# Tail pairs of a mixture of experts added to their nodes by accumulating scatters, with the gathers of the other pairs moved beside them

## The chip, the cores and the metric

The kernel runs on one core of one Trainium2 chip. The metric is the time of one execution on the device, in microseconds. The kernel before takes 3260.33 us (median of 14 runs, 3238.46 to 3288.77). The engines are named as the profile names them: PE (TensorE matmuls), PEld (its weight loads), DVE (VectorE), ACT (ScalarE), POOL (GpSimd), SP (SyncE, which here only issues DMAs).

## What is computed

A block of a graph network over 6250 nodes of 256 features (float32) with 100000 edges. Cut to its outline:

```python
xn = _layernorm(x)
x = x + _L0_gnn_ref(xn, edge_index, ...) + _L0_mix_ref(xn[None], ...)[0]
x = x + _L0_ffn_ref(_layernorm(x)[None], ...)[0]

# _L0_gnn_ref: relu(gcn) and relu(gat); each is a segment sum over the edges of rows fetched by source
# _L0_mix_ref: linear attention, 8 heads of 64
# _L0_ffn_ref:
gate_scores = x @ Wg + bg
_, idx = jax.lax.top_k(gate_scores, 2)               # two of 8 experts for every node
mask = jax.nn.one_hot(idx, 8).sum(axis=-2)
h = gelu(einsum('td,edh->teh', x, W1) + b1)          # H = 512
y = einsum('teh,ehd->ted', h, W2) + b2
out = einsum('ted,te->td', y, mask)                  # the two experts' rows are added, unweighted
```

The change concerns the last line: each node's output is its row `x` plus the rows that its two experts return.

## The kernel before

The nodes lie in NB = 49 blocks of P = 128 rows (the last has 106). Most of the time goes to the two graph layers and the mix: POOL fetches rows of neighbours by indirect DMA, PE adds them up per block of destination nodes. None of that is edited, except for the size of one ring of buffers.

The second graph layer finishes blocks one after another, and the class `Experts` works on finished blocks inside it. `finish` computes a block's `x2` and stores it in the array x2d in memory; groups of blocks are then normalised (`normed`), gated, and every node gets two slots, one in the region of each of its experts. `put` (L774) scatters the normalised rows to their slots in the array xs, one indirect DMA for each block and each of the two experts, 98 in all, issued by POOL.

A *pair* is 256 consecutive rows of one expert's region (a pair of 128-row tiles). At most 56 pairs can be needed, and at least 49 (`NPAIR`, `SURE`). For each pair:

- `pick` (DVE) chooses which pair is full, on small tables on the device; its number goes into `pairs`.
- `load` (SP) loads its rows `xg` (256 KB) and its expert's two weight matrices `w1q`, `w2q` (512 KB each).
- `enter` (PE, DVE) transposes the rows, `inner` (PE, ACT) makes the hidden layer with its gelu, `outer` (PE, DVE) multiplies back, half by half, and adds the bias into `yb` (L897). `yb` has two buffers.
- SP stores `yb` as pair number q of the array ys (L903).

The layer's order is written out by hand, slot by slot: each slot issues its gathers, some of the experts' products from the list `todo` (with a budget) and the results that are due. `add` and `after` file a step with a lag in slots. When the layer ends, `order.close()` ends that regime, and `rest` runs: what is left, issued as a plain program that the scheduler of the framework orders at build time by the dependencies between the steps. Each engine then executes its instructions in that fixed order. 36 pairs are picked inside the layer; 20 are left to `rest`, the tail.

`rest` writes rows of zeros behind the last row of each region (SP, L926), so that a pair that is not full reads zeros, and picks and computes the remaining pairs. `turn` (L959) turns each node's slot in xs into a place in ys: pairs were taken in an order that only the device knows, so DVE compares each slot's pair with the 56 entries of `pairs` (L974), multiplies by the entry's number (L978) and sums (L979), for 49 blocks at a time, twice. Then for each block: SP loads `x2d` into `o` (L943), POOL fetches the two rows of each node from ys (L946, 98 indirect DMAs), DVE adds them to `o` (L956) and SP stores the block (L957). Every one of these gathers waits for every store of a pair:

```python
for store in self.stores:
    tc.add_manual_dep(back.ins, store.name, ..., reason="every pair is stored")
```

The graph layers' gathered rows lie in `xres`, an SBUF tile with a place for every block, and in a second tile `ring`. After the layer neither is used in the kernel before.

## Time and profile before

| what | us |
|---|---|
| median of 14 runs | 3260.33 (3238.46 to 3288.77) |
| profiled execution, its own time | 3260.22 |
| span of that execution | 3258.4 |
| busy PE, DVE, ACT, POOL in the span | 2078.2, 1475.8, 755.0, 1594.0 |
| granted PE clock, mean | 0.813 |
| start of the last scatter of rows (L774) | 2914.8 |
| first and last issue of the tail's 20 stores (L903) | 2930.8, 3107.8 |
| first of the 98 gathers (L946) | 3111.0 |

How to read what follows. The page gives the busy time of each engine over the whole span and in 40 slices. The view of windows gives, for stretches that one chooses, each engine's busy time with its number of instructions, the clock that PE was granted (1.00 is full), the mean share of time in which the 16 DMA engines were busy, and the rate that they moved. In the view of groups a line names the source line, the engine, the operation, the tile written and the tile read, their shapes, the number of instructions, then busy microseconds in all, mean nanoseconds of one, and the idle time ahead of them with what ended it. The timeline gives the start of each instruction, its duration, and in brackets how long its engine had been idle and what released it. Averages over the span say little here, since the kernel's end consists of stages with different limits.

### The profile page before, as it was taken

The page shows a single profiled execution, that of the slowest core. Times are in us where ns is not written, and L with a number is a line of the kernel's source. Part 1 is how long each engine was busy: PE and PEld are TensorE (multiplying, and loading weights), DVE is VectorE, ACT ScalarE, POOL GpSimd, SP SyncE. Part 2 cuts the span into 40 slices and gives each one's busy share as a digit, 9 for nine tenths or more (in the row PEclk, how much of TensorE's full clock was granted, in tenths as well). Part 3 has the DMA queues.
Part 4 walks back from the last instruction along what each step waited for, and adds up shares of the span by engine and source line. Part 5 has one row for each costly group of instructions (what it writes and reads, how often), then busy time and mean ns, then how long its engine had stood idle before and what let it go on. Part 6 is the DMA issues. An engine that isn't in the chain of part 4 may idle for free. (4 is left out here: it accounts for less than half of the span.)

```text
span 3258.4 us, 34185 instructions
## 1 busy us (share of the span) xinstructions
PE 2078.2 (64%) x9260; PEld 1530.1 (47%) x9261; DVE 1475.8 (45%) x5122; ACT 755.0 (23%) x1914; POOL 1594.0 (49%) x1753
## 2 busy tenths in 40 slices
PE   3572766776678675642474557786886878678710
PEld 2451444454445454532353335564665657457610
DVE  6221433443433323363654555475655656552322
ACT  3230111222222110011111223342433434221100
POOL 1036666666563625626056666555665565210056
PEclk9686888888889887875687778897988889789865
DMA  3443333333334365634254454565556555335455
GB/s 110 123 149 96 103 98 95 99 101 98 91 116 138 110 182 157 181 111 139 73 155 115 131 156 153 173 190 149 183 175 185 159 170 154 105 127 199 153 160 165
DMA packets 299242, 450.27 MB, mean 138 GB/s; under 512 B 44666, under 2 KB 225566, under 8 KB 298879
## 3 DMA queue, kind: packets, MB, share of 16 engines
q0 software_dynamic: 77184, 210.12, 22.9%
q1 hardware_dynamic: 202690, 220.25, 21.3%
q10 hardware_dynamic: 19165, 17.60, 1.8%
q8 instruction: 78, 1.28, 0.2%
q14 instruction: 125, 1.02, 0.1%
HBM read 377.19 MB, written 71.40 MB: 138 GB/s over the span
## 5 line engine op out<-in xcount | busy, mean ns | idle before, releaser
L1554 POOL DMA_INDIRECT xres<-ytab,srcidx x698 | 691.6, 991 | 560.9 <-PE agg L1558 241.1
L1748 POOL DMA_INDIRECT xres<-ftab,srcidx x455 | 449.6, 988 | 356.7 <-PE agg L1882 153.7
L1558 PE MATMUL agg<-xres,S 128*128 128x256 f32 x1396 | 363.4, 413 | 20.2 <-issue 19.9
L1558 PEld LDWEIGHTS agg<-xres,S 128*128 128x128 f32 x1396 | 293.8, 212 | 111.8 <-issue 61.7
L1748 POOL DMA_INDIRECT ring<-ftab,srcidx x243 | 236.3, 972 | 131.5 <-issue 52.8
L1882 PE MATMUL agg<-xres,PW 128*128 128x257 f32 x910 | 273.1, 441 | 30.5 <-issue 15.8
L870 PE MATMUL px<-xT,w1q 128*128 128x256 f32 x896 | 243.1, 425 | 60.8 <-DVE xT L858 32.1
L1875 ACT ACTIVATE PW<-S,z 128x128 f32<-128x128 bf16 x698 | 225.0, 393 | 194.3 <-DVE S L1858 61.9
L434 DVE TENSOR_REDUCE var<-sq 128x16 f32<-128x1024 f32 x49 | 59.8, 1220 | 406.1 <-ACT sq L432 351.0
L870 PEld LDWEIGHTS px<-xT,w1q 128*128 128x128 f32 x896 | 184.0, 213 | 99.0 <-DVE xT L858 36.0
L1882 PEld LDWEIGHTS agg<-xres,PW 128*128 128x128 f32 x910 | 192.9, 220 | 67.3 <-issue 20.2
L892 PE MATMUL px<-w2q,hT 128*128 128x256 f32 x896 | 215.2, 391 | 14.3 <-ACT hT L877 5.9
L946 POOL DMA_INDIRECT yg<-ys,part x98 | 96.3, 983 | 236.7 <-issue 229.9
L774 POOL DMA_INDIRECT xs<-xn,to_i x98 | 100.3, 1023 | 220.3 <-DVE slot L751 194.1
L427 PE MATMUL kv<-wkvT,xnT 128*128 128x512 f32 x392 | 203.1, 666 | 0.1
L892 PEld LDWEIGHTS px<-w2q,hT 128*128 128x128 f32 x896 | 170.0, 194 | 43.8 <-ACT hT L877 6.8
L877 ACT ACTIVATE hT<-px,b1T 128x256 f32<-128x256 f32 x224 | 95.5, 472 | 323.0 <-PE px L870 200.9
L1782 PE MATMUL pm<-Q,lift_i 128*128 128x512 bf16 (+1 forms) x200 | 77.4, 387 | 139.3 <-DVE mt L1794 97.6
L453 PE MATMUL dots<-kk,vv 128*128 128x128 f32 x392 | 66.9, 323 | 142.3 <-DVE vv L446 76.7
L897 DVE TENSOR_TENSOR yb<-px,fb 128x256 f32<-128x256 f32 x112 | 44.6, 421 | 243.2 <-PE px L892 145.9
L1794 DVE TENSOR_REDUCE mt<-pm 128x1 f32<-128x384 f32 (+1 forms) x201 | 122.1, 608 | 42.8 <-remote 18.9
L1882 PE MATMUL agg<-ring,PW 128*128 128x257 f32 x486 | 133.4, 415 | 3.5 <-issue 3.5
(359 smaller groups left out, 3313.4 us busy)
## 6 DMA issues: line engine op xcount, KB each, us to landing
w1q<-in_L_ffn_W_dram SPq DMA_DIRECT2D x56, 512.0 KB
w2q<-in_L_ffn_W_dram SPq DMA_DIRECT2D x56, 512.0 KB
xg<-xs SPq DMA_DIRECT2D x56, 256.0 KB
ys<-yb SPq DMA_DIRECT2D x56, 256.0 KB
F<-ftab SPq DMA_DIRECT2D x14, 899.5 KB
Y<-ytab SPq DMA_DIRECT2D x14, 896.0 KB
xnT<-xnTd SPq DMA_DIRECT2D x98, 128.0 KB
xres<-ytab,srcidx POOLq DMA_INDIRECT x698
```

What stands on the lines that cost most here:

```text
L427: nc.tensor.matmul(kv[:, s, :], xnT[:, k, :], wkvT[:, k, s * INNER : (s + 1) * INNER], start=(k == 0), stop=(k == 1),)
L774: put = nc.gpsimd.indirect_dma_start(out=xs[:, :], out_offset=bass.IndirectOffsetOnAxis(ap=to_i[:n, j, k : k + 1], axis=0), in_=bt["xn"][k ...
L870: nc.tensor.matmul(ph, w1q[:, k, c * P : (c + 1) * P], xT[:, k, :], start=(k == 0), stop=(k == 1))
L877: nc.scalar.activation(hT[:, c0 + c, :], ph, AF.Gelu, bias=self.b1T[:, c0 + c, bass.ds(e, 1)], scale=1.0)
L892: nc.tensor.matmul(py, hT[:, c, j * P : (j + 1) * P], w2q[:, c, :], start=(c == 0), stop=(c == HC - 1))
L946: back = nc.gpsimd.indirect_dma_start(out=yg[:n, :], out_offset=None, in_=ys[:, :], in_offset=bass.IndirectOffsetOnAxis(ap=self.slot[:n, j ...
L1554: nc.gpsimd.indirect_dma_start(out=R, out_offset=None, in_=ytab[:, :], in_offset=bass.IndirectOffsetOnAxis(ap=srcidx[:, t : t + 1], axis=0),)
L1558: nc.tensor.matmul(sums[b], hot[s][:, t - t0, :], R, start=(t == first[b]), stop=(t == first[b + 1] - 1))
L1748: nc.gpsimd.indirect_dma_start(out=ch["R"][c], out_offset=None, in_=ftab[:, :], in_offset=bass.IndirectOffsetOnAxis(ap=srcidx[:, ch["t0"] ...
L1794: nc.vector.tensor_reduce(ch["mt"][:, q : q + 1], ch["pm", q][:, :w, :].rearrange("p c e -> p (c e)"), AX.X, ALU.max)
L1875: nc.scalar.mul(PW[:, c - c0, :], ch["S", q][:, c - c0, :], ch["z"][:, c : c + 1])
L1882: nc.tensor.matmul(ch["pa"], ch["PW", q][:, c - c0, :], ch["R"][c][:, 0 : D + 1], start=(c == 0), stop=(c == ch["C"] - 1),)
```

## The change

The tail is the pairs that are picked after the layer; `rest` calls their first number `cut` (the constant FEW = 37 is an upper limit on the pairs picked in the layer).

- The rows of a pair in the tail aren't stored to ys. Each half (128 rows) is added to its nodes' rows in x2d, by an indirect DMA from POOL with `compute_op=ALU.add`. So that the node of a row is known, every row of xs gets a 257th column with the node's number (ACT copies it in `normed`), and DVE copies that column of the pair's `xg` into a tile `whose` with four buffers. Rows of zeros behind a region carry numbers of 256 spare rows at the end of x2d.
- Two such scatters may touch the same row, so each waits until the one before has landed.
- Only the first `cut` pairs are stored in ys, with one pair of zeros behind them. `turn` works on `cut` columns instead of 56; a slot whose pair isn't among them gets the pair of zeros.
- The gathers from ys wait for the stores before the cut only. They go into `xres`, the first row of a node straight (`sums`), the second through `yg` and an add of DVE. They are issued a few at a time between the scatters (`self.backs`), the rest after them.
- At the end 13 steps of four blocks each load x2d, add `sums` and store.
- The ring of the layer has 26 rows of its own instead of 27, for the space.

```diff
+    FEW = 37
...
-    xs = dram.tile([NX * RG, D], FP, name="xs")
-    ys = dram.tile([NPAIR * PAIR, D], FP, name="ys")
+    xs = dram.tile([NX * RG + PAIR, D + 1], FP, name="xs")
+    ys = dram.tile([(NPAIR + 1) * PAIR, D], FP, name="ys")
...
-    x2d = dram.tile([NR, D], FP, name="x2d")
+    x2d = dram.tile([NR + PAIR, D], FP, name="x2d")
...
-            xn = self.fp.tile([P, D], FP, name="xn", bufs=2 * GB + 2)
+            xn = self.fp.tile([P, D + 1], FP, name="xn", bufs=2 * GB + 2)
+            i = bt["i"][k]
+            nc.scalar.copy(xn[:, D:], self.nodes[:, i : i + 1])
...
-            if self.waiting == 2 or len(self.puts) < need:
+            if self.waiting == 2 or len(self.puts) < need or (self.cut is None and self.taken == self.few):
                 return self.after(1, lambda: self.pick(need))
...
-            xg = fp.tile([P, 2, D], FP, name="xg")
+            xg = fp.tile([P, 2, D + 1], FP, name="xg")
...
+                if self.cut is not None and q >= self.cut:
+                    self.whose[q] = self.fp.tile([P, 2], I32, name="whose", bufs=4)
+                    nc.vector.tensor_copy(self.whose[q], xg[:, :, D])
...
+                if q in self.whose:
+                    nc.gpsimd.indirect_dma_start(
+                        out=x2d[:, :], out_offset=bass.IndirectOffsetOnAxis(ap=self.whose[q][:, j : j + 1], axis=0),
+                        in_=yb[:, j, :], in_offset=None, compute_op=ALU.add,
+                    )
+                    for back in self.backs[:4]:
+                        back()
+                    del self.backs[:4]
+                    return
                 if j == 0:
                     return
                 store = nc.sync.dma_start(ys[q * PAIR : (q + 1) * PAIR, :].rearrange("(j p) d -> p j d", p=P), yb)
...
         def rest(self, tp):
+            self.cut = self.taken
+            none = tp.tile([P, 4, D + 1], FP, name="none")
+            nc.vector.memset(none, 0.0)
+            for j in range(4):
+                nc.vector.tensor_scalar(none[:, j, D:], pcol, float(NR + j % 2 * P), None, op0=ALU.add)
+            nc.sync.dma_start(xs[NX * RG :, :].rearrange("(j p) d -> p j d", p=P), none[:, 0:2, :])
+            nc.sync.dma_start(x2d[NR:, :].rearrange("(j p) d -> p j d", p=P), none[:, 0:2, 0:D])
+            store = nc.sync.dma_start(
+                ys[self.cut * PAIR : (self.cut + 1) * PAIR, :].rearrange("(j p) d -> p j d", p=P), none[:, 0:2, 0:D]
+            )
...
-            while self.taken < NPAIR:
+            for _ in range(8):
                 self.clock += 1
                 self.products(6.0)
                 self.results()
             self.turn(tp)
+            sums = xres[:, :, 0:D]
+            for i in range(NB):
+                for j in range(2):
+                    self.backs.append(lambda i=i, j=j: self.back(tp, sums, i, j))
             self.drain(6.0)
-            for i in range(NB):
-                n = rows(i)
-                o = tp.tile([P, D], FP, name="o", bufs=4)
-                nc.sync.dma_start(o, x2d[i * P : (i + 1) * P, :])
...
+            for back in self.backs:
+                back()
+            XO = 4
+            for i in range(0, NB, XO):
+                n = min(XO, NB - i)
+                o = tp.tile([P, XO, D], FP, name="o", bufs=4)
+                nc.sync.dma_start(o[:, :n, :], x2d[i * P : (i + n) * P, :].rearrange("(j p) d -> p j d", p=P))
+                nc.vector.tensor_tensor(o[:, :n, :], o[:, :n, :], sums[:, i : i + n, :], op=ALU.add)
...
+        def back(self, tp, sums, i, j):
+            n = rows(i)
+            to = tp.tile([P, D], FP, name="yg", bufs=4) if j else sums[:, i, :]
+            back = nc.gpsimd.indirect_dma_start(
+                out=to[:n, :], out_offset=None, in_=ys[: (self.cut + 1) * PAIR, :],
+                in_offset=bass.IndirectOffsetOnAxis(ap=self.slot[:n, j * NB + i : j * NB + i + 1], axis=0),
+            )
+            for store in self.stores:
+                tc.add_manual_dep(back.ins, store.name, ..., reason="every pair before the cut is stored")
+            if j:
+                nc.vector.tensor_tensor(sums[:n, i, :], to[:n, :], sums[:n, i, :], op=ALU.add)
...
         def turn(self, tp):
+            n = self.cut
...
-            same = tp.tile([P, NB, NPAIR], BF, name="same")
+            same = tp.tile([P, NB, n], BF, name="same")
...
-            NR1, NR2 = NB * RW // GW, 27
+            NR1, NR2 = NB * RW // GW, 26
```

## The prediction

> **What bounds the kernel now.** The page's slices first. The first 85% of the span is the layers' work, and the change hardly touches it; what it reorders begins when the layer's last gathers end, near 2808 us. So I cut the rest with the view of windows at the places where the engines change.
>
> ```profile
> core 0: us, PE busy (x) PEld busy (x) DVE busy (x) ACT busy (x) POOL busy (x), PEclk, DMA share, GB/s
> 2808.00:2887.00 79.00, 69.67 (x383) 56.35 (x382) 47.11 (x190) 32.30 (x94) 0.00 (x0) 0.94 0.29 94
> 2887.00:2930.00 43.00, 21.94 (x89) 17.93 (x90) 26.14 (x209) 5.12 (x10) 9.64 (x10) 0.68 0.48 156
> 2930.00:3098.00 168.00, 137.96 (x611) 113.44 (x610) 50.68 (x178) 29.12 (x68) 0.00 (x0) 0.94 0.53 175
> 3098.00:3111.00 13.00, 8.48 (x40) 6.55 (x38) 2.28 (x6) 1.90 (x4) 0.01 (x1) 1.00 0.32 101
> 3111.00:3247.00 136.00, 0.00 (x0) 0.00 (x0) 40.33 (x96) 0.00 (x0) 94.56 (x97) 0.51 0.62 181
> 3247.00:3258.00 11.00, 0.00 (x0) 0.00 (x0) 1.20 (x3) 0.00 (x0) 1.76 (x1) 0.50 0.20 53
> ```
>
> Two stages follow each other with nothing shared: 181 us in which PE multiplies the last pairs and POOL is empty, then 147 us in which POOL fetches and PE is empty. The seam is one wait: every gather waits for the last store of a pair.
>
> ```profile
> L903 SPq DMA_DIRECT2D ys<-yb x20: 360/431/881, 2930.8 to 3107.8; - x20
> ```
>
> Twenty pairs are stored there: the seventh at 2975.3, the seventeenth at 3070.8, so 9.55 us a pair, 4.8 us a half, set by PE (138 of 168 us busy). Then the gathers, in the timeline:
>
> ```profile
> 3110.99 0.98 POOL L946 DMA_INDIRECT yg<-ys,part  x1 [195.23 <-issue]
> 3112.28 0.97 POOL L946 DMA_INDIRECT yg<-ys,part  x1 [0.31 <-issue]
> 3113.55 0.95 POOL L946 DMA_INDIRECT yg<-ys,part  x1 [0.30 <-issue]
> 3113.77 0.43 DVE L956 TENSOR_TENSOR o<-yg,o 128x256 f32<-128x256 f32 x1 [6.01 <-DMA yg<-ys,part]
> ```
>
> One gather costs POOL 0.95 us and 0.30 us before the next, 1.25 in all (with its stalls on o the mean is 136/97 = 1.40). Issue to first use is 3113.77 - 3110.99 = 2.78 us: the only round trip of an indirect DMA seen alone here, and the nearest row to a link of the new chain.
>
> ```profile
> L974 DVE TENSOR_TENSOR same<-pairsb,mine 128x2744 bf16<-128x2744 bf16 x2 | 6.0, 3010 | 0.0
> L979 DVE TENSOR_REDUCE place<-same 128x49 f32<-128x2744 bf16 x2 | 6.0, 3006 | 0.0
> L978 DVE TENSOR_TENSOR same<-same,pairsb 128x2744 bf16<-128x2744 bf16 x2 | 3.1, 1575 | 0.0
> L897 DVE TENSOR_TENSOR yb<-px,fb 128x256 f32<-128x256 f32 x40 | 15.5, 420 | 102.8 <-PE px L892 102.8
> ```
>
> **The change, part by part.** *In the layer.* The limit of 37 doesn't bind: in the order built from either program 36 pairs are picked when the layer ends. So 20 pairs are the tail, and the layer keeps its picks. New there: 49 ACT copies of a column (a fraction of a microsecond each; ACT is busy 32 of 79 us at the layer's end, and each is ready before its DVE norm), rows of 1028 instead of 1024 bytes in the 98 scatters of L774 and the pair loads, and one ring slot of 75 less (a gather may be asked for one slot, about 1.3 us, later). I take 0: POOL's waits on PE (L1748) and ACT's idle time cover them. Without that cover: 49 x 0.2 = 10 us, an estimate.
>
> *Removed.* The 20 stores of the tail (0.43 us of SP each, beside PE), the seam, the 49 loads and 49 stores of 128 KB, and 20/56 of the slot table: DVE's 2 x (3.01 + 1.58 + 3.01) = 15.2 us become 9.7 at 36 columns. But that table now lies amid pair work, and the first gather needs it.
>
> *Added.* 40 accumulating scatters, each held by the landing of the one before and by DVE's yb; POOL's queue waits with it, the gathers behind it too. DVE gets 20 small copies of node numbers and 49 adds of gathered rows (0.43 us each, 21 us) that stood behind the seam before: it was busy 51 of 168 us, so their time fits, but an add that waits for its gather (up to 2.8 us) holds the yb and xT of a pair behind it; PE is ahead by then, so 0. SP gets three stores of zeros, POOL nothing else. In the built order POOL runs: the layer's 10 last puts, 14 scatters (7 pairs), then one stretch of 98 gathers with 12 scatters (6 pairs) among them, in runs of 4 gathers and three runs of about 20, then the last 14 scatters (7 pairs). yb has two buffers, so PE cannot get more than two pairs ahead of POOL's scatters: behind a run of 20 gathers (25 us) PE stands.
>
> *The link.* Let L be the time from one scatter to the next in the chain. No row has an accumulating DMA. Lower bound 2.8, the gather's round trip; upper 5.6, twice it, since each row is read as well as written. I take the middle, 4.2: the gather moves the same bytes, but doesn't write where it has read.
>
> A rule speaks against the change here. The Trainium skill ("Collectives: The Full Stack", Why ReduceScatter is half of AllGather) says an add on the way needs two source reads, two descriptors per chunk, and so runs at half the rate of a copy (measured ratio 1.93). No row of this trace shows it; applied to the whole round trip it would make L 5.4 and the sum below about 3296.
>
> *Stations, on the clock of the profiled span.*
> 1. First gather. Scatters begin at 2931 as the stores did: 2931 + 14 x 4.2 = 2989.8; by the other path, seventh pair 2975.3 + table 9.7 + one link 4.2 = 2989.2. So 2990 (2988 at L = 2.8, 3009 at 5.6).
> 2. The stretch is POOL's: 110 x 1.25 = 138, and 12 x 0.4 = 5 for scatters dearer to issue (an estimate between 0 and the 0.95 of a second issue): 143, to 3133. The chain is no limit in it (12 links, 50 us). PE gets six pairs, 57 us, in 143 us: some 85 us are lost against before.
> 3. The last seven pairs. Two lie ready in yb: 4 x 4.2 = 17. Five come at PE's pace: 48. To 3198. From L = 4.8 the chain is the slower one: 14 x 5.6 = 78. PE was three fifths idle, and the windows show its clock at 0.68 where it is half busy against 0.94 where it is full; at 0.81 in between the 48 us become 56: +8, to 3206 (from 0).
> 4. Landing of the last scatter: one link, 3210.
> 5. The final stage. 13 loads of 512 KB, an add each (4 x 0.43 = 1.7 us), 14 stores, all behind the last scatter: 12.8 MB. The best 20 us in the tail move 308 GB/s, which makes 42; the gathers' stage made 181, which makes 71. Large blocks and nothing between are nearer the first: 260, 49 us. Around it: first load 5 (o waits up to 5.2), one add 1.7, the last store 5.2 (the last add ends at 3253.2, the span at 3258.4): 12. To 3271.
> 6. The profiled execution is 3260.22 for a span of 3258.4, and the median 3260.33: +1.9. Sum: **3273**.
>
> So the 150 us behind the last store (3108 to 3258) become 65, and the last pair ends 98 us later, at 3206: a loss of 13.
>
> One more rule, beside the sum: the skill ("DMA: Bandwidth & Descriptors", Rules for kernel authors) says that an accumulating DMA beside another access of the same bytes can lose a write, hence one must wait for the other. The trace of before cannot show this; the built order obeys it, with a wait in every scatter. Were it not needed, L would be one issue, 1.3 to 1.7 us, and the sum about 3255, since PE and POOL set the rest.
>
> **The rivals.**
> - *The chain sets the pace.* L above 4.8 us. At 5.6: 3009 + 143 + 78 + 6 + 61 + 1.9 = 3299 (the chain hides the clock's loss); each further microsecond adds 29, so 6.5 us gives 3325. For it: a read and a write in series, and transfers of weights and rows beside them (DMA share 0.53). Against: PE's 4.8 us a half hides all below it.
> - *An add at a copy's price.* L = 2.8 and no dearer issue: 2988 + 138 + 59 + 8 + 3 + 61 + 1.9 = 3259: no change. PE's starvation and the saved stage cancel. Nothing in the trace prices the add, so nothing is against it but the bytes.
> - *Faster: POOL's stretch is shorter.* If the 0.30 us between gathers goes, since more are out at once to different buffers, 98 x 0.30 = 29 us go from station 2: 3244. It decides from 0.23 us a gather (3250). Against: the gap is there after scatters and gathers alike. For: these gathers go into tiles that are free, without the waits on o.
> - *The gathers are hidden after all* would need PE to run on: 13 pairs in the stretch instead of 6, seven x 9.6 = 67 us less, 3206. The two yb buffers exclude it in the built order.
>
> **How the numbers follow.** A difference of 0.3% (10 us) is about what a measurement of this kernel can tell from none: 3250 to 3270 is the same. My case (3262 to 3295) 0.48, of which 0.10 fall below 3270; the chain 0.22, all slower; the copy's price 0.13, the same; the short stretch and anything else to that side 0.17, faster. So faster 0.17, same 0.23, slower 0.60. Range: the low end has L = 2.8, no dearer issue, no loss of clock, 308 GB/s: 2988 + 138 + 59 + 3 + 54 + 1.9 = 3244. The high end has the chain's 3299, with 181 GB/s (+22) 3321, and half a microsecond more of L (+14): 3335. Beyond them about 0.1 on either side.
>
> **What would show it.** Right: no PE work for about 20 us at a time between 2990 and 3133 with POOL at its 1.25 us; PE waiting on yb for POOL's scatter; 20 pairs of the tail ending near 3200; a last stage of 60 us without POOL; 36 columns in the table (128x1764). Wrong: scatters over 4.8 us apart where POOL has nothing else (the chain), or a PE that works through the gathers' stretch. What would break the sum altogether: a layer that ends other than at 2887, or x2d loads that start before the last scatter.

## The result, and the profile after

The changed kernel takes 3295.83 us (median of 10 runs, 3285.18 to 3311.17) against 3257.6 us for the kernel before in the same comparison: ratio 1.0122, interval 1.010 to 1.0144, so 38 us slower. The forecast was 13 us slower, in a range of 3244 to 3335: the direction and the range held, the size was a third of the measured one.

Its profiled execution has a span of 3286.1 us. Executions of one program differ by some 20 us in the layers already (the first layer, which nothing of the change touches, ended at 1406 us in this profile and at 1428 in the one before), so from here on times in the tail are counted from the start of the layer's last aggregation matmul: 2885.7 us in the profile before, 2858.3 in this one. I call the time from there to the end the tail. It was 372.7 us and is 427.9: 55 us more; the 17 us between that and the 38 measured must be gained ahead of it, in the layers. Three more profiles of the changed kernel gave 426.1, 426.4 and 428.5.

The view of windows over the tail of the changed kernel, cut where the engines change:

```profile
core 0: us, PE busy (x) PEld busy (x) DVE busy (x) ACT busy (x) POOL busy (x), PEclk, DMA share, GB/s
2858.00:2990.00 132.00, 79.34 (x313) 64.49 (x313) 58.07 (x354) 15.53 (x35) 31.32 (x24) 0.74 0.57 154
2990.00:3156.00 166.00, 56.93 (x195) 43.94 (x194) 28.40 (x77) 8.76 (x20) 114.57 (x110) 0.65 0.50 134
3156.00:3239.00 83.00, 57.17 (x242) 46.55 (x241) 10.89 (x30) 12.63 (x28) 21.68 (x14) 0.85 0.44 100
3239.00:3286.00 47.00, 0.00 (x0) 0.00 (x0) 15.13 (x13) 0.00 (x0) 0.00 (x0) 0.50 0.85 273
```

The stages are the ones that were forecast. Seven pairs go ahead of the first gather (14 scatters); then come 98 gathers and 12 scatters in 166 us, with PE busy a third of the time; then the last seven pairs in 83 us; then 47 us of loads and stores. Beside the forecast, in microseconds after the layer's last aggregation:

| | forecast | profile |
|---|---|---|
| first gather | 104 | 132 |
| length of POOL's stretch | 143 | 166 |
| last seven pairs, with the last landing | 77 | 83 |
| last stage | 61 | 47 |
| tail | 385 | 428 |

The groups of the tail that answer to the rows shown of before:

```profile
L918 POOL DMA_INDIRECT x2d<-yb,whose x40 | 62.7, 1567 | 157.0 <-DVE yb L912 75.0 <-DMA x2d<-yb,whose 28.5 <-DVE whose L874 19.7
L1012 DVE TENSOR_TENSOR xres<-yg,xres 128x256 f32<-128x256 f32 (+1 forms) x49 | 20.2, 423 | 84.2 <-DMA yg<-ys,part 82.2 <-issue 2.0
L1030 DVE TENSOR_TENSOR same<-pairsb,mine 128x1764 bf16<-128x1764 bf16 x2 | 4.0, 1990 | 0.0
L1035 DVE TENSOR_REDUCE place<-same 128x49 f32<-128x1764 bf16 x2 | 4.0, 1980 | 0.0
L1034 DVE TENSOR_TENSOR same<-same,pairsb 128x1764 bf16<-128x1764 bf16 x2 | 2.1, 1073 | 0.0
```

The table has 36 columns (36 x 49 = 1764) and takes 10.1 us, near the 9.7 worked out. The new row is the scatter: 1.57 us of POOL each against 0.98 for a gather, and 157 us in which POOL stood ahead of one. The timeline shows its links. First two where little else is loaded, then the first ones of the tail:

```profile
3212.28 1.54 POOL L918 DMA_INDIRECT x2d<-yb,whose  x1 [3.46 <-DVE yb L912]
3216.84 1.54 POOL L918 DMA_INDIRECT x2d<-yb,whose  x1 [3.02 <-DVE xT L870]
3221.41 1.54 POOL L918 DMA_INDIRECT x2d<-yb,whose  x1 [3.02 <-DMA x2d<-yb,whose]
...
2903.32 1.61 POOL L918 DMA_INDIRECT x2d<-yb,whose  x1 [15.22 <-DVE yb L912]
2912.89 1.56 POOL L918 DMA_INDIRECT x2d<-yb,whose  x1 [7.97 <-DVE xT L870]
2920.37 1.54 POOL L918 DMA_INDIRECT x2d<-yb,whose  x1 [5.91 <-DMA x2d<-yb,whose]
2929.29 1.54 POOL L918 DMA_INDIRECT x2d<-yb,whose  x1 [7.37 <-DVE yb L912]
2938.99 1.54 POOL L918 DMA_INDIRECT x2d<-yb,whose  x1 [8.16 <-DVE yb L912]
```

3212.28 to 3216.84 is 4.56 us. The first four links are 9.6, 7.5, 8.9 and 9.7 us. The releaser in the brackets is only the semaphore that came last; the packets of the transfers tell what the waits are made of. A quiet scatter's first packet starts 2.1 us after the issue begins and its last ends at 3.4; for that of 2903.32 it is 5.2 and 8.5. In all four of these links the next half lay ready in yb before the last packet had ended. The window from 2903.3 to 2912.9 has the DMA engines full, with weights being loaded, at 272 GB/s; the quiet one from 2943.5 to 2948.0 has 29 GB/s.

And the break in POOL's stretch, in the timeline of POOL, ACT and PE:

```profile
3062.15 0.94 POOL L1001 DMA_INDIRECT yg<-ys,part  x1 [0.30 <-issue]
3077.41 1.60 POOL L918 DMA_INDIRECT x2d<-yb,whose  x1 [14.32 <-DVE yb L912]
...
3062.03 0.47 ACT L892 ACTIVATE hT<-px,b1T 128x256 f32<-128x256 f32 x1 [69.94 <-remote]
...
3040.05 5.49 PE L885 MATMUL px<-xT,w1q 128*128 128x256 f32 x12 [2.82 <-issue]
3062.56 2.08 PE L885 MATMUL px<-xT,w1q 128*128 128x256 f32 x4 [17.01 <-issue]
```

POOL ends a run of 21 gathers and then waits 14.3 us for a pair that isn't there. PE's last 12 matmuls before it are on record from 3040 to 3045.5, but ACT, which waits for these products, starts only at 3062.03, when the run of gathers ends. A second wait, of 11.2 us, lies behind the last gather (3155.8 to 3167.0), so in the time of the last seven pairs.

The last stage, in the timeline and in a row of the view of windows:

```profile
3238.56 1.52 SPq L987 DMA_DIRECT2D o<-x2d  x3
3242.47 1.23 DVE L988 TENSOR_TENSOR o<-o,xres 128x1024 f32<-128x1024 f32 x1 [16.35 <-DMA o<-x2d]
```

```profile
3245.00:3275.00 30.00, 0.00 (x0) 0.00 (x0) 11.21 (x10) 0.00 (x0) 0.00 (x0) 0.50 1.00 324
```

From the first load to the end it takes 47.5 us. From 3245 to 3275 the loads and stores move 324 GB/s, with the DMA engines full.

### The profile page after: what moved, and what is told of

Same layout as the page of the kernel before. It is cut to its first block, busy times and chain, and to the rows that moved or that the text cites. A ratio compares the mean times of both kernels' runs of the same rounds, so it can differ in the third digit from the quotient of the medians.

```text
span 3286.1 us, 34111 instructions
## 1 busy us (share of the span) xinstructions
PE 2111.6 (64%) x9260; PEld 1553.4 (47%) x9261; DVE 1465.4 (45%) x5104; ACT 759.6 (23%) x1962; POOL 1653.6 (50%) x1794
## 5 line engine op out<-in xcount | busy, mean ns | idle before, releaser
L1806 POOL DMA_INDIRECT xres<-ftab,srcidx x464 | 457.2, 985 | 361.5 <-PE agg L1940 156.2
L885 PE MATMUL px<-xT,w1q 128*128 128x256 f32 x896 | 253.1, 441 | 87.5 <-DVE xT L870 37.2
L1806 POOL DMA_INDIRECT ring<-ftab,srcidx x234 | 227.6, 973 | 129.7 <-issue 49.6
L907 PE MATMUL px<-w2q,hT 128*128 128x256 f32 x896 | 225.4, 403 | 71.9 <-DVE yb L912 38.2
L885 PEld LDWEIGHTS px<-xT,w1q 128*128 128x128 f32 x896 | 192.5, 222 | 130.0 <-DVE xT L870 43.1
L1940 PEld LDWEIGHTS agg<-xres,PW 128*128 128x128 f32 x928 | 195.0, 218 | 59.1 <-issue 14.7
L918 POOL DMA_INDIRECT x2d<-yb,whose x40 | 62.7, 1567 | 157.0 <-DVE yb L912 75.0
```

What stands on the lines that cost most here:

```text
L885: nc.tensor.matmul(ph, w1q[:, k, c * P : (c + 1) * P], xT[:, k, :], start=(k == 0), stop=(k == 1))
L907: nc.tensor.matmul(py, hT[:, c, j * P : (j + 1) * P], w2q[:, c, :], start=(c == 0), stop=(c == HC - 1))
L1806: nc.gpsimd.indirect_dma_start(out=ch["R"][c], out_offset=None, in_=ftab[:, :], in_offset=bass.IndirectOffsetOnAxis(ap=srcidx[:, ch["t0"] ...
L1940: nc.tensor.matmul(ch["pa"], ch["PW", q][:, c - c0, :], ch["R"][c][:, 0 : D + 1], start=(c == 0), stop=(c == ch["C"] - 1),)
```

## The experiments

The sets ran on several chips. On one of them (the runs e1_plain, e2_nogather, e3_late, e4_order) the kernel before takes 2700.6 us, on the others 3233 to 3258; ratios are compared within a set only. The tail hardly depends on it where both were tried: 411.1 and 411.2 us for e3, 381.4 and 380.8 for e4, 331.8 and 328.7 for e2. So the tails are what I compare, and after them the ratios. The kernel before was profiled once; its tail is that of the first set.

| run | last scatter | tail | ratio to the kernel before, interval |
|---|---|---|---|
| kernel before | (last store 222) | 373 | 1 |
| changed, four profiles | 374 to 377 | 426 to 428.5 | 1.0122, 1.010 to 1.0144; 1.0137, 1.009 to 1.0184; 1.0135, 1.0097 to 1.0173; 1.0171, 1.0105 to 1.0236 |
| e1_plain | 326 | 376 | 1.002, 0.9997 to 1.0043 |
| e2_nogather | 279, again 277 | 332, 329 | 0.9845, 0.9808 to 0.9882; again 0.9797, 0.9756 to 0.9838 |
| e3_late | 268, again 268 | 411, 411 | 1.0186, 1.0153 to 1.0218; again 1.010, 1.0059 to 1.0142 |
| e4_order | 330, again 329 | 381, 381 | 1.0043, 1.0017 to 1.0069; again 0.9988, 0.9949 to 1.0026 |
| e5_yb4 | 374 | 425 | 1.0159, 1.0114 to 1.0203 |
| e6_end | (last store 232) | 377 | 0.9954, 0.9922 to 0.9985 |
| e7_early | 328 | 379 | 0.9961, 0.9928 to 0.9995 |
| e8_pair | 314, again 312 | 366, 365 | 0.9924, 0.9895 to 0.9954; again 0.9941, 0.9913 to 0.9968 |
| e9_pair_nogather | 253 | 305 | 0.9736, 0.9701 to 0.9771 |
| e11_noadd | 367 | 419 | 1.0114, 1.0077 to 1.015 |
| e12_ring | (last store 221) | 370 | 0.995, 0.9924 to 0.9976 |

My theory after the result was that two things hold the pairs: the gathers in POOL's queue (theory A), and the chain of scatters, which the forecast had thought hidden (theory B).

**What an accumulating scatter costs.**

```diff
-                        in_=yb[:, j, :], in_offset=None, compute_op=ALU.add,
+                        in_=yb[:, j, :], in_offset=None,
```

> The 40 scatters write their rows instead of adding them (the computation changes there: a node's row is replaced by the tail pair's row); each still waits for the one before. In the changed kernel a link takes 4.5 us where nothing else loads (1.54 us to issue, landing at 3.4, the next one released at 4.25) and 7.4 to 9.7 us where weights are being loaded. Theory A, the add itself is dear (it reads first): the quiet link falls to about 3.2, the issue to 0.96 as in the layer's puts; 28 links lie on the path, so about 30 us less, 3265. Theory B, the link is a round trip and a wait, whatever is carried: link 4.0 or more, at most 12 us less, 3284 or more.

The quiet link falls from 4.5 to 3.15 us, the issue from 1.54 to 0.96:

```profile
2645.26 0.96 POOL L918 DMA_INDIRECT x2d<-yb,whose  x1 [3.21 <-DMA x2d<-yb,whose]
2648.42 0.96 POOL L918 DMA_INDIRECT x2d<-yb,whose  x1 [2.20 <-DMA x2d<-yb,whose]
2651.57 0.96 POOL L918 DMA_INDIRECT x2d<-yb,whose  x1 [2.19 <-DMA x2d<-yb,whose]
```

That is theory A's 3.2 of its expectation. The add has 144 packets where the write has 48, its transport takes 1.30 us instead of 0.52 (packets of the trace, first to last), and its issue 0.58 us more: together the 1.35 us between the links. The other 3.15 of 4.5 us a plain write pays too. The tail of 376 us isn't to be set against 428 for this alone: in this chip's trace the break in POOL's stretch is missing as well. From the first gather to the end of the last it took 2448.4 to 2588.2, 139.8 us, with a run of 20 gathers followed by a scatter at once; one wait of 6.7 us lies behind the last gather.

The rule that was weighed in the prediction (the Trainium skill, "Collectives: The Full Stack", Why ReduceScatter is half of AllGather: an add on the way reads two sources and goes at half a copy's rate) comes near for the transport, where this run shows 2.5 times, and not for the link, of which the transport is under a third: 4.5 us against 3.15 is 1.43 times.

**The pairs without gathers.**

```diff
             for i in range(NB):
-                for j in range(2):
-                    self.backs.append(lambda i=i, j=j: self.back(tp, sums, i, j))
+                if i == 0:
+                    nc.vector.memset(sums, 0.0)
+                    self.backs.append(lambda: self.back(tp, sums, 0, 0))
```

> 97 of the 98 gathers and their adds are left out (the rows of the pairs before the cut are missing from the output); scatters and ending stay. Counted from the layer's last aggregation matmul, the changed kernel has its last scatter at +377 and its end at +428. Theory A, the gathers starve the pairs: without them the pairs go at PE's 9.6 us, last scatter near +45 + 205 = +250, end near +300, 3168 us. Theory B, the chain of scatters is what holds the pairs (mean of its first 14 links 6.2 us): 40 x 6.2 = 248, last scatter near +293, end near +343, 3211 us.

> 97 of 98 gathers and their adds left out, once more, as the measure for the next run. Last scatter near +279, tail near 332, mean link 5.8 us.

Last scatter at 279 and 277, between A's 250 and B's 293; 40 scatters took 223 to 225 us from first to last, a mean of 5.7 us, where the kernel before needed 177 us from first to last store. Each scatter follows the landing of the one before, even where PE is fast. Six of them in the timeline of the second of these runs, and the windows between them:

```profile
2999.90 1.57 POOL L918 DMA_INDIRECT x2d<-yb,whose  x1 [3.84 <-DVE yb L912]
3004.46 1.54 POOL L918 DMA_INDIRECT x2d<-yb,whose  x1 [2.99 <-DVE yb L912]
3012.78 1.54 POOL L918 DMA_INDIRECT x2d<-yb,whose  x1 [6.78 <-DMA x2d<-yb,whose]
3017.26 1.54 POOL L918 DMA_INDIRECT x2d<-yb,whose  x1 [2.94 <-DVE whose L874]
3021.80 1.54 POOL L918 DMA_INDIRECT x2d<-yb,whose  x1 [3.00 <-DVE yb L912]
3026.31 1.54 POOL L918 DMA_INDIRECT x2d<-yb,whose  x1 [2.96 <-DVE xT L870]
```

```profile
2999.90:3004.50 4.60, 4.16 (x21) 3.22 (x19) 1.37 (x4) 0.00 (x0) 1.61 (x2) 1.00 0.37 58
3004.50:3012.80 8.30, 4.98 (x16) 3.96 (x17) 1.58 (x5) 0.47 (x1) 1.52 (x2) 0.79 0.84 252
3012.80:3017.30 4.50, 4.50 (x23) 3.91 (x22) 0.17 (x1) 2.57 (x6) 1.56 (x2) 1.00 0.42 47
3017.30:3021.80 4.50, 4.41 (x22) 3.50 (x20) 0.85 (x2) 0.53 (x2) 1.50 (x1) 1.00 0.53 127
3021.80:3026.30 4.50, 3.46 (x16) 2.62 (x16) 1.27 (x3) 0.00 (x0) 1.54 (x1) 1.00 0.43 60
3026.30:3034.80 8.50, 5.33 (x18) 4.27 (x19) 1.26 (x4) 0.69 (x2) 1.54 (x1) 0.80 0.80 249
```

Three links of 4.5 us and one of 8.4 in every four: the long one is the one beside which the next two pairs' rows and weights come in, at 250 GB/s. Of the 39 links of this run the ten beside which the other queues moved 195 GB/s or more took 7.1 to 9.5 us, and the scatter's first packet started 4.1 to 5.1 us after its issue began; the 29 others, beside 126 GB/s or less, took 4.3 to 6.7, most of them 4.5 with a first packet at 2.1. No run moves the loads away, so that they cause the long links is read from these traces, not tried. Four links make 22 us for two pairs; PE needs 19.

**The chain halved.** Rows of one expert are different nodes, so the two halves of a pair need no order between them.

```diff
+                if j == 0:
+                    return
                 if q in self.whose:
-                    nc.gpsimd.indirect_dma_start(
-                        out=x2d[:, :], out_offset=bass.IndirectOffsetOnAxis(ap=self.whose[q][:, j : j + 1], axis=0),
-                        in_=yb[:, j, :], in_offset=None, compute_op=ALU.add,
-                    )
+                    done = []
+                    for h in range(2):
+                        put = nc.gpsimd.indirect_dma_start(
+                            out=x2d[:, :], out_offset=bass.IndirectOffsetOnAxis(ap=self.whose[q][:, h : h + 1], axis=0),
+                            in_=yb[:, h, :], in_offset=None, compute_op=ALU.add,
+                        )
+                        for one in self.landed:
+                            tc.add_manual_dep(put.ins, one.name, ..., reason="the pair before has landed")
+                        done.append(put.ins)
...
+                    self.landed = done
```

> As the kernel without gathers, but the two halves of a pair are scattered one behind the other after the second half, and the second doesn't wait for the first (rows of one expert are different nodes); each pair still waits for the pair before: 20 links instead of 40. Theory B, the chain sets the pace of the pairs: they fall back to PE's 9.6 us, last scatter near +47 + 19 x 9.6 + 12 = +242 instead of +279, tail near 295. Theory C, the pace comes from the loads that the scatters delay, not from their chain: last scatter at +265 or later.

```profile
3064.00 1.54 POOL L922 DMA_INDIRECT x2d<-yb,whose  x1 [5.15 <-DVE yb L913]
3067.40 1.54 POOL L922 DMA_INDIRECT x2d<-yb,whose  x1 [1.86 <-DVE yb L913]
3076.14 1.54 POOL L922 DMA_INDIRECT x2d<-yb,whose  x1 [7.19 <-DMA x2d<-yb,whose]
3077.98 1.54 POOL L922 DMA_INDIRECT x2d<-yb,whose  x1 [0.30 <-DVE whose L875]
```

Here the wait of 3064.00 is one for yb, not for a landing, and 3077.98 follows 3076.14 at once. First to last scatter takes 199 us, 24 less than with 40 links on the same chip, and the tail goes from 329 to 305. So the chain did set a part of the pace, as theory B says: of the 46 us between 223 and the 177 of the kernel before, the halved chain gives back 24. The last scatter at 253 lies between B's 242 and C's 265, so what holds the other 22 us isn't decided; the long link beside the loads is still in the path (3067.40 to 3076.14).

**Gathers after the pairs.**

```diff
-                    for back in self.backs[:4]:
-                        back()
-                    del self.backs[:4]
                     return
```

(with POOL's instructions of the tail kept in the order of the program)

> All 98 gathers come after the last scatter. Theory A (gathers among the pairs starve PE and win nothing): last scatter near +250 from the layer's end, 98 x 1.25 = 123 us of gathers, ending 47: +423, 3291 us, the same as the changed kernel within 10 us. Theory B (the chain is slow by itself): last scatter near +293, 3334 us. If the overlap of gathers and pairs were worth what it was meant to, this kernel would be some 60 us or more slower than the changed one.

> All gathers after the last scatter. On the chip of the first set its tail was 411 us. If the overlap of gathers and pairs in the changed kernel is worth nothing: the same as the changed kernel within 15 us, or less. If it is worth what POOL does among the pairs (12 scatters' worth of 165 us), 40 us or more slower than it.

With no gathers among the pairs the tail is 411 us, 15 to 17 less than with them, and the ratio in the same set is 1.010 against 1.0171. This kernel has another overlap instead, which the changed one lacks: since the last scatter has landed, the blocks of x2d are loaded, added to and stored while the gathers run, and only 12 us lie behind the last gather, where the changed kernel has 47 behind its last landing. Against the run without gathers, the gathers add 427 - 330 = 97 us to the changed kernel's tail where POOL's time for them is 123. So its overlap hides 26 us of gathers, and gives up some 35 us of overlap at the end.

**POOL's order.** The scheduler had put the gathers in three runs of about 20. Here POOL keeps the program's order.

```diff
-            self.drain(6.0)
-            for back in self.backs:
-                back()
+            with tc.manual_schedule(engines={POOL}):
+                self.drain(6.0)
+                for back in self.backs:
+                    back()
```

> POOL's instructions of the tail stay in the order of the program: after the first 13 scatters, 4 gathers behind each scatter, 3 scatters at the end; nothing else is changed. Theory A, the runs of 20 gathers starve PE through the two buffers of yb: each half pair then takes 1.9 + 4 x 1.25 = 6.9 us of POOL, last scatter near +132 + 25 x 6.95 + 14 = +320 from the layer's end instead of +377, some 57 us less, 3239 us. Theory B, gathers slow the pairs wherever they stand (DVE's adds that wait for them, loads beside them): less than 20 us gained, 3276 or more.

> POOL in the order of the program, 4 gathers behind each scatter after the first 13. If the runs of 20 gathers are what holds the pairs: last scatter near +330, tail near 381 as on the chip where the kernel before takes 2700, 45 us less than the changed kernel. If not: within 15 us of it.

```profile
3008.45 1.61 POOL L918 DMA_INDIRECT x2d<-yb,whose  x1 [0.30 <-issue]
3010.36 0.99 POOL L1002 DMA_INDIRECT xres<-ys,part  x1 [0.30 <-issue]
3011.66 1.06 POOL L1002 DMA_INDIRECT yg<-ys,part  x1 [0.30 <-issue]
3013.02 0.95 POOL L1002 DMA_INDIRECT xres<-ys,part  x1 [0.31 <-issue]
3014.28 0.95 POOL L1002 DMA_INDIRECT yg<-ys,part  x1 [0.30 <-issue]
3015.71 1.61 POOL L918 DMA_INDIRECT x2d<-yb,whose  x1 [0.48 <-issue]
```

Last scatter at 330 where 320 was expected; again at 329, with a tail of 381, 47 us less than the changed kernel beside it (428). Four gathers fill the link: most scatters go out at once, and about every fourth waits 3 to 4 us for a yb that was written 0.3 us before. The stretch of gathers becomes longer, 192 us instead of 165, but 24 scatters lie in it instead of 12, and three are left behind it instead of 14: from the last gather to the last scatter it takes 10 us instead of 79. So the same scatters and gathers, spread, cost the tail 8 us against the kernel before, and in runs 55.

**Two buffers or four.**

```diff
-                    yb = self.fp.tile([P, 2, D], FP, name="yb")
+                    yb = (self.tp or self.fp).tile([P, 2, D], FP, name="yb", bufs=4 if self.tp else 2)
```

> The changed kernel with four buffers of yb in the tail instead of two (and eight of whose); POOL's order is the same. Theory A, the two buffers of yb starve PE behind the runs of 20 gathers: PE gets two more pairs ahead, 2 x 9.6 = 19 us less than the changed kernel. Theory B, the chain of scatters (mean link 5.8 us without any gather) and POOL's order set the pace, PE has time to spare: within 8 us of the changed kernel.

Nothing: 425 us. A run of gathers is still followed by a break of 14.7 us. So the two buffers of yb, which the prediction names as the reason why PE stands behind a run, don't hold it by themselves. What PE waits for is in this run's timeline of DVE and of PE:

```profile
3008.18 0.43 DVE L1014 TENSOR_TENSOR xres<-yg,xres 128x256 f32<-128x256 f32 x1 [2.05 <-DMA yg<-ys,part]
3008.53 0.42 DVE L913 TENSOR_TENSOR yb<-px,fb 128x256 f32<-128x256 f32 x1
...
3011.50 5.49 PE L908 MATMUL px<-w2q,hT 128*128 128x256 f32 x12 [30.02 <-DVE yb L913]
```

PE stands 30 us for adds into yb for which a buffer is free: seven pairs have been scattered, this is the eighth, and there are four buffers. The adds stand in DVE's order behind others that each wait for a gather. The changed kernel's two waits of this kind, 14.4 and 16.4 us, read the same way. Four buffers without those other adds weren't tried together. And as long as POOL's order leaves 14 scatters behind the last gather, each a link of 4.5 us or more, pairs that are ready sooner could save the two breaks and little else.

**DVE's order.**

```diff
-            if j:
-                nc.vector.tensor_tensor(sums[:n, i, :], to[:n, :], sums[:n, i, :], op=ALU.add)
```

> The adds of DVE on the gathered second rows are left out (the second expert's row is missing from the output where its pair lies before the cut); all gathers stay. Theory D, DVE's order: its adds wait for gathers (82 us of waiting in the stretch) and hold yb and xT behind them; without them POOL's stretch falls from 165 to about 146 and pairs lie ready behind it, last scatter near +340 instead of +375. Theory E, PE's late updates or the order of POOL hold the pairs: last scatter within 8 us of +375.

> The changed kernel, as the measure for the other three: tail of 426 us after the layer's last aggregation where the kernel before takes 3230 us or more; where it takes 2700 and PE's updates don't come late, the stretch without its holes of 14 and 11 us, tail near 395.

The break shrinks from 14.6 to 10.9 us and the last scatter comes at 367 instead of 377. DVE's adds, which wait for gathers in its order, hold the pairs a little: 10 of the 47 us, at the edge of what was set for theory E.

What remains of the breaks goes together with updates of PE that come late, an update being the signal by which PE tells a waiting engine that a product is done. In e11, where DVE's adds are gone, the timeline of PE and of ACT ahead of the break has this:

```profile
3003.60 5.02 PE L885 MATMUL px<-xT,w1q 128*128 128x256 f32 x12 [2.13 <-issue]
3017.89 0.47 ACT L892 ACTIVATE hT<-px,b1T 128x256 f32<-128x256 f32 x1 [32.63 <-remote]
```

PE's products are on record until 3008.6, and ACT, which waits for them, starts 9.3 us later; for the second half of the same pair's products it is 11.6 us (3035.6 to 3047.2). Waits for PE that end more than 3 us after the end on record stand in the tail of each of the four profiles of the changed kernel seven to nine times, in e5 eight and in e11 eleven times; there is none in e2_again, e4_again, e7, e8 and e9. So they go with the long runs of gathers. SP's small register steps take up to 0.7 us there instead of 0.04. On the chip of the first set (kernel before 2700 us) there is none in the whole program, and e1 there had no break behind the first run. All this is read from traces: no run takes the late updates away and leaves POOL's order and the chip as they are. What delays them wasn't found.

> The changed kernel once more, beside the others of this set. On the chip of the last set the layers ran faster (kernel before 2700.6 us), the tail did not. If the whole difference lies in the tail, the kernels differ by the same microseconds as before, +38 (ratio 1.014 at 2700). In the tail, counted from the layer's last aggregation: last scatter near +377, end near +428 against +373 in the kernel before. If the two holes of 14 and 11 us in POOL's stretch belong to the first chip alone, the difference is nearer +15.

> The changed kernel beside the others of this set. Where PE's updates come late while POOL gathers without a break (seen where the kernel before takes 3230 to 3260 us): tail of 426 us after the layer's last aggregation, last scatter near +375. Where they don't (the kernel before at 2700): the stretch of gathers without its two holes (14 and 11 us), last scatter near +345, tail near 395.

All three repeats fell on chips where the kernel before takes 3233 us or more: breaks of 14 to 15 us again, tails of 426 to 428.5. The changed kernel itself wasn't measured on the chip without late updates.

**The ending alone.** No scatters; 56 columns; sums in xres and blocks of four.

```diff
-            self.cut = self.taken
+            self.cut = NPAIR
...
-            for _ in range(8):
+            while self.taken < NPAIR:
```

> No scatters: all 56 pairs are stored and gathered as before, after the last store; only the new way of gathering (first row straight into sums, adds among themselves, x2d in blocks of four) is kept, with the longer rows of xs. The gathers' stage of the kernel before lasts 136 + 11 us for 98 x 1.25 = 123 us of POOL. If the ending by itself is worth its part, the stalls on o go: 123 + 10 = 133, some 15 us less than before (2685 where before is 2700). If not, the same as before within 5 us. Nothing of it can be slower than before by 10 us unless the longer rows cost something in the layer.

The tail is 377, not 358: the last store comes 10 us later than before and the gathers' stage still takes 377 - 235 = 142 us, some 6 less than before where 15 were expected. The expected 15 us are in the ratio (0.9954) all the same, but not in the tail; the next run says where they are from.

**The ring.** The kernel before with one number changed.

```diff
-            NR1, NR2 = NB * RW // GW, 27
+            NR1, NR2 = NB * RW // GW, 26
```

> The kernel before with 26 rows in the layer's second ring instead of 27, nothing else. If the layer's gain of 10 to 20 us comes from the other rotation of the ring: ratio near 0.9955 where the kernel before takes 3230 us or more. If it comes from elsewhere (the copies of node numbers, the longer rows, chance): within 0.15% of the kernel before.

Ratio 0.995, interval 0.9924 to 0.9976: the smaller ring makes the kernel before 16 us faster (8 to 25), with the tail as before (370). In the one profile the second layer, from the first layer's end to its own last aggregation, takes 1433.5 us instead of 1457.9; the two profiles are of different sets, and the first layer, which the ring doesn't touch, differs by 11 us as well. Why a slot less is better wasn't tried.

**Versions.** The table made as soon as all slots are known, the order written out, 2, 2, 2 and 5 gathers behind four scatters:

```diff
-                    for back in self.backs[:4]:
+                    n = (2, 2, 2, 5)[self.scattered % 4]
+                    self.scattered += 1
+                    for back in self.backs[:n]:
                         back()
-                    del self.backs[:4]
+                    del self.backs[:n]
```

> The changed kernel with the table made as soon as every node has its slots, and POOL's order written out: behind every scatter 2, 2, 2, 5 gathers in turn, so that the gathers stand in the time in which POOL waits for the landing of a scatter (a quiet link has 4.5 - 1.9 = 2.6 us for them, one beside loads of weights 6.6). Theory B (the chain sets the pace and its waits have room for every gather): 40 links of 5.8 us, last scatter near +45 + 232 = +277, end near +328, 45 us less than the kernel before (2655). Theory A (gathers hold the pairs wherever they are): last scatter at +330 as with 4 behind each, the same as before or slower.

Last scatter at 328, near theory A's 330, though POOL's own time for the tail, 40 x 1.9 + 98 x 1.25 = 199 us, fits between 50 and 249. Then this together with both halves at once:

> The gathers again, 2 behind the first half's scatter and 3 behind the second's, the table early, 20 links instead of 40. POOL needs 2 x 1.9 + 5 x 1.25 = 10.1 us for a pair, PE 9.6. Theory B: 20 x 10.1 = 201 us and some waits for links beside loads, last scatter near +265, tail near 318, some 55 us less than the kernel before. Theory A, gathers among the pairs hold PE whatever the chain does: last scatter near +325 as with the order of 2, 2, 2, 5 and 40 links, tail near 378, the same as the kernel before.

> The version with halves scattered together and 5 gathers for each pair, once more: ratio to the kernel before 0.992 as measured in four runs; tail near 366 us.

Last scatter at 314 and 312, nearer to A's 325 than to B's 265; tails of 366 and 365, ratio 0.9924 and 0.9941: a little faster than the kernel before (0.6 to 0.8%), and faster than the changed one. Of its 19 to 25 us some 16 are the ring's, 7 the tail's; it isn't to be told from the kernel before with the smaller ring (0.995). A pair takes 13.5 us in it where POOL needs 10.1 and e9, without gathers, takes 10.2; so gathers among the pairs cost even when they are spread and the chain is short. By the profile POOL waits on every second pair, some 3.5 us for its yb and 2.8 us more ahead of its second half; what holds the pair there stayed open.

## Why the prediction was right and wrong

Right: that POOL's order has three parts and PE starves in the middle one, that the end becomes shorter (forecast 85 us, measured 99) and the pairs end later by more (forecast 98, measured 154), and so the sign. The account closes with the measured terms: forecast +13; first gather 28 later, stretch 23 longer, last pairs 6 longer, last stage 14 shorter makes +56 (the profiles: +55); the ring -16, if it is worth in the changed kernel what it is in the kernel before; together +40, measured +38.

- **The link ("I take the middle, 4.2") was mis-sized where loads run.** The runs showed 4.5 us alone. Beside loads at 205 to 272 GB/s it is 7.5 to 10, and that is one link in four, and all of the first four. The bounds of 2.8 and 5.6 came from a gather that had the memory nearly to itself (47 GB/s from 3111 to 3113.8); the stage in which the scatters were put runs at 175 GB/s on average and at 308 in places, which the windows of before showed. The mean without gathers, 5.7, lies above the 4.8 from which the prediction itself says that the chain becomes the slower one. The first 13 links take 85 us, a mean of 6.5, and all but some 3 us of what lies above 4.5 are late landings. This is station 1's 28 us, and the first rival's condition was met: it had 0.22. Its sum of 3299 came near the measured time by luck: its stretch is 23 us short, its last stage 14 long, and the ring's 16 us aren't in it.
- **The stretch (143).** POOL's own time in it was right: e1, with plain scatters and without late updates, took 139.8 us where the forecast without dearer scatters has 138. The scatters' dearer issue was 0.66 us each instead of 0.4. Of the 23 us above, 14 are the one break in it, POOL waiting for a pair, where the prediction has PE waiting for POOL; 3 are the dearer issue, and 5 to 6 small waits and longer issues, most of them at the last three gathers. The step "yb has two buffers, so PE cannot get more than two pairs ahead" named the wrong reason: four buffers changed nothing, PE stood for adds of DVE that lie behind waits for gathers, and POOL's order alone was worth 47 us. Why the break is there stays open, beyond its going with late updates of PE.
- **"Two lie ready in yb"** was wrong: none was (11.2 us of waiting behind the last gather). Station 3 with its landing came out near all the same, 83 against 77, by luck in its parts: where the forecast has 17 us of ready pairs and 56 at PE's pace, there are 11 of waiting and 68 at the chain's pace, with two links of nearly 9 beside loads.
- **The last stage (61)** was mis-sized by its rate: 324 GB/s, not the 260 between two rows. Big blocks with nothing between them went beyond the best row of before, 308.
- **The ring, costed at nothing** with a bound of +1.3 us, was worth -16 in the kernel before. No gain had been let in.
- **The faster rival** (0.30 us less between gathers) fell: the gap is 0.30 or 0.31 us ahead of 106 of the stretch's 110 instructions. The rival of the hidden gathers fell too, though not by yb's buffers.
- Two small slips move nothing: the seventh store of before starts at 2975.7, not 2975.3, and a link of 5.4 us makes the stations' sum 3293, not 3296.

## What to carry to other kernels

Price a chain of DMAs, each of which waits for the one before, by the link under the traffic that will run beside it, not by one that had the memory to itself; and if the chain is near the engine's pace, shorten it by what the data guarantee (halves with different rows) before overlapping anything. When work is moved into the idle time of a queue, look at the order that the scheduler makes of it: the same instructions spread evenly made the tail 8 us longer here, and in runs of twenty 55. Change a buffer count that has to give way by itself first; its own effect can be of the size of the whole result.

## What was not expected of the hardware

Updates of PE that come up to 16 us late (ACT at 3062.03 above) and register steps of SP of 0.7 us while POOL issues some twenty gathers without a break, on every chip on which the changed kernel was profiled; none of it is in the traces of the chip on which the kernel before takes 2700 us instead of 3240. In the layers the traces of the slower chips have 230 to 320 updates each that come more than 3 us after the end on record, whatever the kernel, and those of the faster chip none. A link of 4.5 us that becomes 8.4 beside loads at 250 GB/s, though its transport alone is 1.3 us: the time is lost ahead of its first packet, which starts 4 to 5 us after the issue begins instead of 2.1. And a ring with 26 rows that is faster by 0.5% than one with 27.
